# Cross-attention in f32 on one core: queries that lead by two steps, a sliced first block, residuals fetched three ahead and three score buffers in turn

## The chip, the cores and the metric

The kernel runs on one core of a Trainium2 chip. The metric is the device time of one execution in microseconds (us). Three runs of the kernel before are given, and one more execution was profiled.

## The reference

There are 2 sequences of 2048 tokens with 640 channels, and a context of 154 rows of 1024 channels for each. The context's first 77 rows are text and its last 77 rows an image prompt. Each kind has its own key and value weights. There are 20 heads of 32 channels. Every head takes two softmaxes over 77 keys each, one for either kind, and the two results are added. All of it is in f32.

```python
q = split(x @ Wq.T)
k, v       = split(text @ Wk.T),    split(text @ Wv.T)
k_ip, v_ip = split(ip @ Wk_ip.T),   split(ip @ Wv_ip.T)
out = attend(q, k, v) + attend(q, k_ip, v_ip)     # softmax(q k^T / sqrt(32)) v
return merge(out) @ Wo.T + bo + x
```

## The kernel before

Inputs come with the contracted dimension first (the launch code transposes them on the host), so tiles hold channels on the partitions. The 4096 tokens are four blocks `j` of 1024, and the 640 channels are five chunks `c` of 128, that is of four heads. A step `m` is one chunk of one block: `m = 5 j + c`, 20 steps in all, and a 21st that only finishes. The schedule is manual: each engine runs its instructions in the order in which the program text emits them, so what is written earlier is queued earlier.

A step makes scores for its 8 token tiles in three groups of 3, 3 and 2 tiles (`GROUPS`). For each group:

- `scores` (L202): TensorE (PE) multiplies queries by keys into four of the eight PSUM banks, `LOW` or `HIGH`. Groups 0 and 1 come at the start of the step, group 2 in its middle.
- `take` (L214): ScalarE (ACT) copies the banks to a buffer `pb` in SBUF. There is one buffer for each group, used again in each step.
- `maxima` (L221, L222): VectorE (DVE) takes the row maxima, GpSimd (POOL) subtracts them.
- `exponential` (L228) on ACT, `sums` (L235, L237) on DVE, `normalise` (L242) on POOL.
- `transpose` (L248) on DVE writes the probabilities, 32x32 blocks transposed, to `tT`.

In the next step `attend` (L260) multiplies values by `tT` into the `LOW` banks, and `take_attention` (L272) copies the result to `aT`. The output product is an object `Out` for each 128 channels by 512 tokens: `fetch` loads its residual from x (L290), `step` does one of its five matmuls (L295), `store` adds product, bias and residual on DVE (L306) and sends the sum out (L309). `fill(n)` does n such matmuls, and `flush` stores those that are complete. `fill` fetches a residual when its output is opened, and the next one with it.

PE's other work is placed into a step in two lists, so that PE has something to do while the softmax runs elsewhere: `after1` stands between the scores of groups 0, 1 and those of group 2, `after2` after `attend`. In block 0 these are the queries of step `m + 1` (`queries`, L177, in two halves `h` of 512 tokens), the values of this step and the keys of the next (`project_kv`, L135). From step 5 on they are query products and `fill(5)`. `turn_to` says which banks these products take in turn.

SP issues all DMAs in the order of the text. The head loads, slice by slice, the first chunk of `wq` and x's first half (L343, L344), then x's second half in one DMA (`load_x`, L164), the context into `wo_ct` (L348), the key and value weights into five slots (L126, `load_w`: each projection sends for the weights five further on) and the rest of `wq` (L355). `spread_v` (L157) copies the transposed values of a chunk to their places in 16 small DMAs; in steps 0 to 4 for sequence 0, in steps 6 to 10 for sequence 1, where they are issued after `take_attention`. x of the next block is loaded at `c == 2`.

Of the kernel before, what the change touches and what calls it, by code (L numbers as in the profile page):

```python
# [8 lines left out]
F32 = mybir.dt.float32  # L9
# [10 lines left out]
def kernel(  # L20
# [43 lines left out]
    OPEN = 4  # L64

    const = ctx.enter_context(tc.tile_pool(name="const", bufs=1))
    qpool = ctx.enter_context(tc.tile_pool(name="qpool", bufs=5))
    small = ctx.enter_context(tc.tile_pool(name="small", bufs=4))
    opool = ctx.enter_context(tc.tile_pool(name="opool", bufs=2))
    rpool = ctx.enter_context(tc.tile_pool(name="rpool", bufs=5))  # L70
    psum = ctx.enter_context(tc.tile_pool(name="psum", bufs=1, space=bass.MemoryType.PSUM))
# [5 lines left out]
    def turn_to(half, n=G):  # L77


        turn[:] = (half[: min(n, G) - 1] + half[-1:]) * 2  # L80

# [10 lines left out]

    pbs = [const.tile([P, n, G, LP], F32, name=f"pb_{t}") for t, n in GROUPS]
    for t in pbs:
        nc.gpsimd.memset(t[:, :, :, 2 * L :], 0.0)
# [92 lines left out]

    def keys_of(s):
        return pbs[s][:, :, :, : 2 * L]  # L190

    def rows_of(s):
        return keys_of(s).rearrange("p n g (t l) -> p (n g) t l", l=L)

# [14 lines left out]

    def take(s, ps):  # L210

        n = GROUPS[s][1]
        for g in range(G):
            nc.scalar.copy(  # L214
                keys_of(s)[:, :, g], ps[g][:, : n * 2 * L].rearrange("p (n l) -> p n l", n=n)
            )

    def maxima(m, s):
        n = GROUPS[s][1] * G
        mx = small.tile([P, n, 2], F32, tag=f"mx{n}", name=f"mx_{m}_{s}")  # L220
        nc.vector.tensor_reduce(mx, rows_of(s), AX.X, ALU.max)  # L221
        nc.gpsimd.tensor_tensor(  # L222
            rows_of(s), rows_of(s), mx.unsqueeze(3).to_broadcast([P, n, 2, L]), ALU.subtract
        )

    def exponential(m, s):
        e = keys_of(s).rearrange("p n g l -> p (n g) l")
        nc.scalar.activation(e, e, AF.Exp, scale=SCALE)  # L228
# [3 lines left out]
    def sums(m, s):  # L232
        n = GROUPS[s][1] * G
        den = small.tile([P, n, 2], F32, tag=f"den{n}", name=f"den_{m}_{s}")
        nc.vector.tensor_reduce(den, rows_of(s), AX.X, ALU.add)  # L235
        rden = small.tile([P, n, 2], F32, tag=f"rden{n}", name=f"rden_{m}_{s}")
        nc.vector.reciprocal(rden, den)  # L237
        rdens[s] = rden

    def normalise(m, s):  # L240
        n = GROUPS[s][1] * G
        nc.gpsimd.tensor_tensor(  # L242
            rows_of(s), rows_of(s), rdens[s].unsqueeze(3).to_broadcast([P, n, 2, L]), ALU.mult
        )

    def transpose(m, s):
        first, n = GROUPS[s]
        nc.vector.transpose(  # L248
            tT[:, first : first + n].rearrange("p n g k s -> p (n g k s)"),
            pbs[s].rearrange("p n g l -> p (n g l)"),  # L250
        )
# [63 lines left out]
    def fill(n, most=OPEN):  # L315


        while n > 0:
            o = next((o for o in opened if o.k < attended[o.j]), None)
            if o is None:  # L320
                v = len(finished) + len(opened)
                if v == NV or len(opened) == most or attended[outs[v].j] == 0:
                    return
                for o in outs[v : v + 2]:
                    o.fetch()
                opened.append(outs[v])
                continue
            o.step()
            n -= 1
            if o.k == NC:  # L330
                opened.remove(o)
                finished.append(o)
# [3 lines left out]
    def flush():  # L336
        for o in finished[len(stored) :]:
            o.store()
            stored.append(o)


    for k in range(NC):
        nc.sync.dma_start(out=wq[:, k, :P], in_=WqT[ts(k, P), :P])  # L343
        nc.sync.dma_start(out=xs[0][:, k, :TB], in_=xT[ts(k, P), :TB])  # L344
    load_x(0, 1)
    half = NCC // 2
    for k in (0, half):
# [4 lines left out]
        load_w()  # L352

    def load_wq(lo, hi):
        nc.sync.dma_start(  # L355
            out=wq[:, :, lo * P : hi * P],
            in_=WqT[:, lo * P : hi * P].rearrange("(k p) o -> p k o", p=P),
        )

    load_wq(1, 2)  # L360
    load_w()
    load_w()
    load_w()
    load_wq(2, NC)
    nc.sync.dma_start(out=bo_sb, in_=bo.rearrange("(c p) -> p c", p=P))
    turn_to(HIGH)
    for h in range(NH):
        queries(0, h)
    for t in range(2):
        project_k(0, t)  # L370

    for m in range(NM + 1):
        j, c, _ = block_of(m)
        new = m < NM
        old = m >= 1
        last = m == NM - 1

        if m < NC:
            after1 = [lambda: queries(m + 1, 0)]
            after1 += [lambda t=t: project_v(m, t) for t in range(2)]  # L380
            after2 = [lambda t=t: project_k(m + 1, t) for t in range(2) if m + 1 < NC]
            after2 += [lambda: queries(m + 1, 1)]
        elif c == 0 and new:
            after1 = [lambda h=h: queries(m + 1, h) for h in range(NH)]
            after2 = [lambda: fill(NC)] * 2
        elif last:
            after1 = [lambda: fill(NC)]
            after2 = [lambda: fill(NC)] + [lambda: fill(NC - 1)] * OPEN
        elif new:
            after1 = [lambda: fill(NC), lambda: queries(m + 1, 0)]  # L390
            after2 = [lambda: fill(NC), lambda: queries(m + 1, 1)]
        else:
            after1 = after2 = [lambda: None]
        flush()
        if new:
            for g, half in ((0, LOW), (1, HIGH)):
                scores(m, g, half)
            for g, half in ((0, LOW), (1, HIGH)):
                take(g, half)
        turn_to(LOW, len(after1))  # L400
        if old:
            transpose(m - 1, 2)
        if new:
            maxima(m, 0)
            maxima(m, 1)
        if c == 2 and j + 1 < NBLK:
            for h in range(NH):
                load_x(j + 1, h)

        ahead = len(after1) - (c > 0 or m == 0)  # L410
        for work in after1[:ahead]:
            work()
        flush()
        if new:
            exponential(m, 0)
            sums(m, 0)
            normalise(m, 0)
        for work in after1[ahead:]:
# [9 lines left out]
        if new:  # L428
            take(2, HIGH)
            maxima(m, 2)  # L430
            exponential(m, 1)
            sums(m, 1)
            normalise(m, 1)
        if old:
            take_attention(m - 1, LOW)
            attended[(m - 1) // NC] += 1
# [8 lines left out]
        if new:  # L445
            exponential(m, 2)
            sums(m, 2)
            normalise(m, 2)
        after2[-1]()
        if m >= NC and c == 0:  # L450
            flush()
        if new:
            transpose(m, 1)
# [38 lines left out]
```

## Time and profile before

| | us |
|---|---|
| three runs, median (lowest, highest) | 549.3 (548.97, 550.48) |
| the profiled execution's own time | 550.32 |
| its span, first to last instruction | 548.5 |
| PE busy | 524.3 (96% of the span) |
| DVE busy | 378.3 (69%) |
| POOL busy | 350.7 (64%) |
| ACT busy | 245.1 (45%) |
| idle time of PE that a profile row gives to a DMA of x | 6.3 |
| idle time of PE given to the output addition (L306), two waits | 9.1 |

The span leaves out what lies around the first and last instruction, which is 1.8 us here. In the profile PE stands for matmuls and PEld for weight loads, which overlap them. An f32 matmul leaves two records. L and a number is the line of the kernel, and SPq is the queue of DMA issues on SP. The granted clock (PEclk) is the share of full speed that TensorE was given.

### The profile page before, as it was taken

The page shows a single profiled execution, that of the slowest core. Times are in us where ns is not written, and L with a number is a line of the kernel's source. Part 1 is how long each engine was busy: PE and PEld are TensorE (multiplying, and loading weights), DVE is VectorE, ACT ScalarE, POOL GpSimd, SP SyncE. Part 2 cuts the span into 40 slices and gives each one's busy share as a digit, 9 for nine tenths or more (in the row PEclk, how much of TensorE's full clock was granted, in tenths as well). Part 3 has the DMA queues.
Part 4 walks back from the last instruction along what each step waited for, and adds up shares of the span by engine and source line. Part 5 has one row for each costly group of instructions (what it writes and reads, how often), then busy time and mean ns, then how long its engine had stood idle before and what let it go on. Part 6 is the DMA issues. An engine that isn't in the chain of part 4 may idle for free.

```text
span 548.5 us, 12745 instructions
## 1 busy us (share of the span) xinstructions
PE 524.3 (96%) x5600; PEld 285.9 (52%) x5600; DVE 378.3 (69%) x285; ACT 245.1 (45%) x441; POOL 350.7 (64%) x129
## 2 busy tenths in 40 slices
PE   5999999999999999999969999999999999969997
PEld 2676676866455445554535455554545544434442
DVE  0077778777798787878667887878588787864121
ACT  1254565546544446454435355464445645450000
POOL 0077967869678795786739595876779668691000
PEclk9999999999999999999979999999999999969999
DMA  7964384400420532121031621111032111121141
GB/s 267 305 185 104 87 271 106 126 17 20 166 78 29 176 127 84 45 65 57 16 106 40 232 70 47 41 39 39 2 98 58 40 39 41 38 99 38 59 165 66
DMA packets 49768, 50.60 MB, mean 92 GB/s; under 512 B 5168, under 2 KB 33712, under 8 KB 49712
## 3 DMA queue, kind: packets, MB, share of 16 engines
q1 hardware_dynamic: 49712, 49.78, 30.2%
q8 instruction: 44, 0.72, 0.6%
q14 instruction: 12, 0.10, 0.1%
HBM read 36.00 MB, written 10.49 MB: 85 GB/s over the span
## 4 chain that ended last, share of the span: by engine, by line
PE 86%; POOL 3%; SPq 3%; DMA 2%; DVE 2%; ACT 1%; issue 1%; ACTq 0%; DVEq 0%; POOLq 0%
PE bank L295 31%; PE bank L177 28%; PE bank L260 13%; PE bank L202 9%; PE bank L135 6%; DMA aT<-in_L_xattn_Wk_ip_dram 2%; POOL pb L242 2%; POOL pb L222 1%; SPq L348 1%; SPq L157 1%; DVE den L235 1%; DMA res<-in_x_dram 1%; DVE mx L221 1%; ACT pb L228 1%; DVE ot L306 0%
## 5 line engine op out<-in xcount | busy, mean ns | idle before, releaser
L222 POOL TENSOR_TENSOR pb<-pb,mx 128x1848 f32<-128x1848 f32 (+1 forms) x60 | 175.6, 2941 | 110.9 <-DVE mx L221 110.9
L242 POOL TENSOR_TENSOR pb<-pb,rden 128x1848 f32<-128x1848 f32 (+1 forms) x60 | 176.2, 2942 | 39.9 <-DVE rden L237 29.7
L177 PE MATMUL bank<-x,wq 128*128 128x512 f32 x400 | 181.9, 603 | 6.3 <-DMA x<-in_x_dram 6.3
L295 PE MATMUL bank<-aT,wo_ct 128*128 128x512 f32 x400 | 182.4, 608 | 2.1 <-ACT pb L214 1.2
L235 DVE TENSOR_REDUCE den<-pb 128x24 f32<-128x1848 f32 (+1 forms) x60 | 111.6, 1859 | 73.3 <-ACT pb L228 73.3
L228 ACT ACTIVATE pb<-pb 128x1848 f32<-128x1848 f32 (+1 forms) x60 | 95.2, 1587 | 97.7 <-POOL pb L222 97.6
L221 DVE TENSOR_REDUCE mx<-pb 128x24 f32<-128x1848 f32 (+1 forms) x60 | 109.2, 1848 | 37.2 <-ACT pb L214 35.9
L177 PEld LDWEIGHTS bank<-x,wq 128*128 128x128 f32 x400 | 75.8, 192 | 99.5 <-issue 94.7
L295 PEld LDWEIGHTS bank<-aT,wo_ct 128*128 128x128 f32 x400 | 75.0, 193 | 95.5 <-issue 85.0
L248 DVE STREAM_TRANSPOSE tT<-pb 128x1920 f32<-128x1920 f32 (+1 forms) x60 | 115.6, 1931 | 7.5 <-POOL pb L242 5.2
L214 ACT COPY pb<-bank 128x462 f32<-128x462 f32 (+1 forms) x240 | 101.5, 528 | 25.0 <-PE bank L202 15.8
L260 PE MATMUL bank<-tT,v 32*32 32x256 f32 x3200 | 71.8, 395 | 6.0 <-DVE ot L306 4.4
L185 ACT COPY qT<-bank 128x512 f32<-128x512 f32 x40 | 23.4, 585 | 95.5 <-PE bank L177 95.5
L202 PEld LDWEIGHTS bank<-kT,qT 32*128 32x128 f32 x1280 | 45.5, 186 | 32.4 <-issue 19.1
L306 DVE SCALAR_TENSOR_TENSOR ot<-bank,bo_sb,res 128x512 f32<-128x512 f32 x40 | 29.5, 739 | 47.1 <-PE bank L295 37.9
L202 PE MATMUL bank<-kT,qT 32*128 32x154 f32 x1280 | 55.4, 306 | 5.0 <-DVE ot L306 4.7
L260 PEld LDWEIGHTS bank<-tT,v 32*32 32x32 f32 x3200 | 46.8, 104 | 24.8 <-issue 6.6
L135 PEld LDWEIGHTS bank<-wo_ct,aT 128*128 128x128 f32 x320 | 43.1, 188 | 5.8 <-issue 3.4
L135 PE MATMUL bank<-wo_ct,aT 128*128 128x154 f32 x320 | 44.7, 295 | 1.0 <-ACT pb L214 0.5
L272 ACT COPY aT<-bank 128x256 f32<-128x256 f32 x80 | 24.3, 391 | 26.9 <-PE bank L260 26.9
L237 DVE RECIPROCAL rden<-den 128x24 f32<-128x24 f32 (+1 forms) x60 | 17.2, 286 | 2.1
L142 ACT COPY kT<-bank 128x154 f32<-128x154 f32 x10 | 2.9, 291 | 15.9 <-PE bank L135 15.9
(9 smaller groups left out, 7.3 us busy)
## 6 DMA issues: line engine op xcount, KB each, us to landing
res<-in_x_dram SPq DMA_DIRECT2D x40, 256.0 KB, 3.5
out_dram<-ot SPq DMA_DIRECT2D x40, 256.0 KB, 2.4
x<-in_x_dram SPq DMA_DIRECT2D x7, 1280.0 KB, 8.6
v<-vS SPq DMA_DIRECT2D x160, 20.0 KB, 1.8
aT<-in_L_xattn_Wk_dram SPq DMA_DIRECT2D x5, 512.0 KB, 6.8
aT<-in_L_xattn_Wk_ip_dram SPq DMA_DIRECT2D x5, 512.0 KB, 4.5
aT<-in_L_xattn_Wv_dram SPq DMA_DIRECT2D x5, 512.0 KB, 5.6
aT<-in_L_xattn_Wv_ip_dram SPq DMA_DIRECT2D x5, 512.0 KB, 4.2
```

Source lines behind the costliest of these rows:

```text
L135: nc.tensor.matmul(out, loaded[n][:, k, :], cT[:, k, :, t, :], start=(k == 0), stop=(k == NCC - 1))
L177: nc.tensor.matmul(pq, wq[:, k, ts(c, P)], xs[j % 2][:, k, ts(h, TB)], start=(k == 0), stop=(k == NC - 1),)
L202: nc.tensor.matmul(ps[g][:, ts(t, 2 * L)], qTs[(m, h)][g * D : (g + 1) * D, ts(st, P)], kT[g * D : (g + 1) * D, c, b].rearrange("p t l -> ...
L214: nc.scalar.copy(keys_of(s)[:, :, g], ps[g][:, : n * 2 * L].rearrange("p (n l) -> p n l", n=n))
L221: nc.vector.tensor_reduce(mx, rows_of(s), AX.X, ALU.max)
L222: nc.gpsimd.tensor_tensor(rows_of(s), rows_of(s), mx.unsqueeze(3).to_broadcast([P, n, 2, L]), ALU.subtract)
L228: nc.scalar.activation(e, e, AF.Exp, scale=SCALE)
L235: nc.vector.tensor_reduce(den, rows_of(s), AX.X, ALU.add)
L242: nc.gpsimd.tensor_tensor(rows_of(s), rows_of(s), rdens[s].unsqueeze(3).to_broadcast([P, n, 2, L]), ALU.mult)
L248: nc.vector.transpose(tT[:, first : first + n].rearrange("p n g k s -> p (n g k s)"), pbs[s].rearrange("p n g l -> p (n g l)"),)
L260: nc.tensor.matmul(pa[r][g * D : (g + 1) * D, : NT * D], v4[rows, c, g, k, :], tT[rows, :, g, k, :], start=(k == 0), stop=(k == NK - 1),)
L295: nc.tensor.matmul(self.po, wo[:, self.k, ts(self.o, P)], aTs[self.j % 2][:, self.k, ts(self.h, TB)], start=(self.k == 0), stop=(self.k == ...
```

## The change

It has four parts, and some reordering that goes with them.

1. Queries of a block's first half (`h = 0`) are made two steps ahead, those of the second half one step ahead as before (`LEAD`). The first products of the kernel become (0,0), (0,1) and (1,0).
2. In the head the five slices of `wq` are issued on ACT's queue, and SP issues both halves of x in five slices each. The second chunk of `wq` goes ahead of the context, and the third comes before the values' weights.
3. A residual is fetched at the store of the output three before it (`FETCH`); its pool has 4 buffers instead of 5.
4. The wide score buffers of groups 0 and 1 are three, taken in turn over the steps; group 2 keeps its own.

The reordering: x of the next block is loaded at `c == 1`. In steps 0, 18 and 19 (`short`) the second maxima come after the work of `after1` and the first two groups are exponentiated after the copies of group 2. In steps 5, 6, 11, 16 and 19 (`late`) the transposes of the step before come after the new maxima. In steps 1 and 2 all of `after1` is queued ahead of the first exponential. In step 18 the last output is stored at the step's end.

```diff
+    LEAD = (2, 1)
+    FETCH = 3
-    rpool = ctx.enter_context(tc.tile_pool(name="rpool", bufs=5))
+    rpool = ctx.enter_context(tc.tile_pool(name="rpool", bufs=4))
...
-        turn[:] = (half[: min(n, G) - 1] + half[-1:]) * 2
+        turn[:] = half[:1] if n == 1 else (half[: min(n, G) - 1] + half[-1:]) * 2
...
-    pbs = [const.tile([P, n, G, LP], F32, name=f"pb_{t}") for t, n in GROUPS]
+    wide = [const.tile([P, 3, G, LP], F32, name=f"pb3_{n}") for n in range(3)]
+    narrow = const.tile([P, 2, G, LP], F32, name="pb2")
...
+    def pb_of(m, s):
+        return narrow if s == 2 else wide[(2 * m + s) % 3]
...
+    def soften(m, s):
+        exponential(m, s)
+        sums(m, s)
+        normalise(m, s)
...
-                for o in outs[v : v + 2]:
-                    o.fetch()
+                outs[v].fetch()
...
         for o in finished[len(stored) :]:
             o.store()
             stored.append(o)
+            for o in outs[len(stored) : len(stored) + FETCH]:
+                o.fetch()
...
     for k in range(NC):
-        nc.sync.dma_start(out=wq[:, k, :P], in_=WqT[ts(k, P), :P])
-        nc.sync.dma_start(out=xs[0][:, k, :TB], in_=xT[ts(k, P), :TB])
-    load_x(0, 1)
+        nc.scalar.dma_start(out=wq[:, k, :P], in_=WqT[ts(k, P), :P])
+    for h in range(NH):
+        for k in range(NC):
+            nc.sync.dma_start(out=xs[0][:, k, ts(h, TB)], in_=xT[ts(k, P), ts(h, TB)])
+    load_wq(1, 2)
...
-    for h in range(NH):
-        queries(0, h)
+    for m, h in ((0, 0), (0, 1), (1, 0)):
+        queries(m, h)
+    turn_to(HIGH, NH)
...
+    def plan(m):
+        q = [lambda h=h: queries(m + LEAD[h], h) for h in range(NH)]
+        out = lambda: fill(NC)
+        if m < NC:
+            v = [lambda t=t: project_v(m, t) for t in range(2)]
+            k = [lambda t=t: project_k(m + 1, t) for t in range(2) if m + 1 < NC]
+            return q[:1] + v, k + q[1:]
+        if m == NM - 1:
+            return [out], [out] + [lambda: fill(NC - 1)] * OPEN
+        if m == NM - 2:
+            return [out], [out, q[1]]
+        if m % NC == 0:
+            return q, [out] * 2
+        return [out, q[0]], [out, q[1]]
+
+    def is_late(m):
+        return m in (NC, NM - 1) or (m > NC and m % NC == 1)
...
+        ahead = len(after1)
+        if ahead > 1 and 2 < m < NM - 2 and c > 0:
+            ahead -= 1
+        short = new and (len(after1) == 1 or m == 0)
+        late = is_late(m)
+        if old and not late:
             transpose(m - 1, 2)
         if new:
             maxima(m, 0)
+        if late:
+            transpose(m - 1, 1)
+        if new and not short:
             maxima(m, 1)
-        if c == 2 and j + 1 < NBLK:
+        if late:
+            transpose(m - 1, 2)
+        if c == 1 and j + 1 < NBLK:
             for h in range(NH):
                 load_x(j + 1, h)
...
         if new:
-            exponential(m, 0)
-            sums(m, 0)
-            normalise(m, 0)
+            if short:
+                maxima(m, 1)
+            else:
+                soften(m, 0)
...
             maxima(m, 2)
-            exponential(m, 1)
-            sums(m, 1)
-            normalise(m, 1)
+            if short:
+                soften(m, 0)
+                if old:
+                    take_attention(m - 1, LOW)
+            soften(m, 1)
...
-        after2[-1]()
-        if m >= NC and c == 0:
+        for work in after2[-1:]:
+            work()
+        if m >= NC and (c == 0 or m == NM - 2):
             flush()
-        if new:
+        if new and not is_late(m + 1):
             transpose(m, 1)
```

## The prediction

> **What bounds the kernel now.** I read the page first, then PE's own waits, then the timeline around each of those waits, then busy time and clock by stretches.
>
> From the page, the busy table and the rows of tenths:
>
> ```profile
> span 548.5 us, 12745 instructions
> PE 524.3 (96%) x5600; PEld 285.9 (52%) x5600; DVE 378.3 (69%) x285; ACT 245.1 (45%) x441; POOL 350.7 (64%) x129
> PE   5999999999999999999969999999999999969997
> PEclk9999999999999999999979999999999999969999
> ```
>
> PE (TensorE matmuls) is the bound; the others have a quarter or more of the span free. The dents are at the start, near slice 21 (274 to 288 us) and slice 36 (480 to 494 us), and the two later ones are dents of the granted clock too. So a gain can only come from these three places. PE's waits, longest first, say what ended them:
>
> ```profile
> PE bank L177 <- DMA x<-in_x_dram: 6.3, 2, 4.1
> PE bank L202 <- DVE ot L306: 4.7, 1, 4.7
> PE bank L260 <- DVE ot L306: 4.4, 1, 4.4
> PE bank L295 <- ACT pb L214: 1.2, 1, 1.2
> ```
>
> The timeline of the start (start, length, then what ran):
>
> ```profile
> 4.10 7.66 PE L177 MATMUL bank<-x,wq 128*128 128x512 f32 x10 [4.10 <-DMA x<-in_x_dram]
> 13.96 4.56 PE L177 MATMUL bank<-x,wq 128*128 128x512 f32 x10 [2.20 <-DMA x<-in_x_dram]
> 18.35 2.27 PE L135 MATMUL bank<-wo_ct,aT 128*128 128x154 f32 x16
> 21.03 2.37 PE L135 MATMUL bank<-wo_ct,aT 128*128 128x154 f32 x16 [0.40 <-DMA aT<-in_L_xattn_Wk_ip_dram]
> ```
>
> Ten records are one query product (five f32 matmuls, two records each). The first takes 7.66 us, later ones 4.5; then PE waits for x, then for key weights, and step 0 starts only at 23.78. Here PE follows the DMAs. The middle and the tail:
>
> ```profile
> 277.08 1.34 SPq L290 DMA_DIRECT2D res<-in_x_dram  x1
> 281.29 0.75 DVE L306 SCALAR_TENSOR_TENSOR ot<-bank,bo_sb,res 128x512 f32<-128x512 f32 x1 [4.56 <-DMA res<-in_x_dram]
> 282.09 1.90 PE L202 MATMUL bank<-kT,qT 32*128 32x154 f32 x18 [4.67 <-DVE ot L306]
> ...
> 482.64 2.08 DVE L235 TENSOR_REDUCE den<-pb 128x24 f32<-128x1848 f32 x1 [3.19 <-ACT pb L228]
> 484.97 0.65 DVE L306 SCALAR_TENSOR_TENSOR ot<-bank,bo_sb,res 128x512 f32<-128x512 f32 x1
> 485.68 5.17 PE L260 MATMUL bank<-tT,v 32*32 32x256 f32 x136 [4.36 <-DVE ot L306]
> ```
>
> In the middle (scores of step 11) a PSUM bank is not free because the output's last addition has no residual: its load stood on SP behind the 16 copies of v (L157, 266.8 to 277.0). In the tail (attention of step 18) the addition has its data but stands on DVE behind the sums of step 19, which wait for an exponential. Busy time and granted clock (the number before the DMA share) in stretches:
>
> ```profile
> 9.00:14.00 5.00, 2.80 (x6) 0.68 (x4) 0.00 (x0) 0.59 (x1) 0.00 (x0) 1.00 1.04 366
> 14.00:21.00 7.00, 6.63 (x26) 4.00 (x26) 0.00 (x0) 0.88 (x2) 0.00 (x0) 1.00 1.16 311
> 277.00:282.00 5.00, 0.43 (x14) 0.20 (x6) 0.71 (x2) 1.89 (x4) 2.15 (x1) 0.76 0.52 169
> 282.00:292.00 10.00, 9.91 (x34) 5.17 (x35) 8.21 (x6) 3.02 (x5) 4.45 (x2) 0.78 0.25 76
> 486.00:496.00 10.00, 10.00 (x144) 5.34 (x113) 5.43 (x4) 2.33 (x5) 7.94 (x3) 0.57 0.40 134
> ```
>
> After each long wait the clock is halved for a while: 10 x 0.22 = 2.2 us lost in the middle, 10 x 0.43 = 4.3 in the tail.
>
> **The change part by part.** *The head.* PE's work is the same in sum: the query product of step 1, first half, moves from inside step 0 to before the first key projections; each later step does the same product one step earlier, and step 18 has none. What counts is whether it fits where PE waits. Queries (0,0) start with x slice 0, whose issue is now SP's first (0.74 instead of 1.17): nearly as before, end 11.8 at the latest. SP's fourth x slice now waits until the first wq slice has landed [...]; that took 1.8 us from issue, so it goes out near 2.6, ahead of the 4.01 of before; behind it only x slices stand. Queries (0,1) need x's second half, landed at 13.9 in before; in slices all but the last matmul can be done by then: end 14.8. Queries (1,0) need 320 KB of wq now put ahead of the context: 0.33 MB at 311 GB/s is 1.1 us, so 15.1, and they run 4.4 us to 19.5. Keys: the first to 21.7, the second waits for its weights, which land 1.1 later than 21.03, so 22.1 to 24.5; the copy and 0.3 us more start step 0 at 24.8. That is 1.0 later than 23.78 with 4.5 us of work less outstanding: gain 3.5.
>
> [...] x's second half went as one 1280 KB DMA at up to 366 GB/s in that stretch, and is cut into five of 256 KB. [...] The trace has five x slices already, issued 0.95 apart, and the 16 engines are 0.8 to 1.0 busy from 3 us on with mixed slices at 275 GB/s (4 to 9 us): at that rate 1.31 MB costs 4.8 us instead of 3.6, so at most 1.2. I follow the row and take 0, since wq's narrow slices, not x's, are in that 275, and SP is spared five issues of 0.43.
>
> *Steps 0 to 2.* Value copies on ACT go before the exponential: 0.3 us of small PE waits (0.4 for vT) go. In step 0 the exponentials stand behind the third group's copies, so normalising starts 3.6 us later than now. By the durations (max 2.05, subtract 3.29, exponential 1.75, sum 2.08, multiply 3.29, transpose 2.12) step 0's last transpose ends 7.2 us into step 1, now 5.0; attention needs it at 11.4. Cost 0, cover 4 us; without it attention of steps 1 to 4 would wait.
>
> *Three wide buffers* free ACT's score copies from the previous transposes (1.6 and 0.6 us in steps 5 and 1): ACT is not on the path, 0. The moved transposes of steps 5, 6, 11, 16 end near 11 us into the step, the output addition after them 11.8 us, while attention asks at about 11.7: 0 to 0.3 each, taken as 0. Loads of the next x block go out one step earlier and still 46 us ahead of use; out stores behind them may be 7 us late, with 11 us between uses of an output buffer: 0.
>
> *The middle.* Each output now fetches the residual three further on, so both residuals of step 10 are issued in step 9, ahead of the 16 copies. The addition then runs when PE ends (about 277), and the scores' 4.7 us wait goes, and the 2.2 of clock: 6.9. Next late is that addition itself: 0 to 0.3.
>
> [...] Rows: 6.8 us at half clock after the middle's wait and 10.2 after the tail's (lost: 2.2 and 4.3 on work). [...]
>
> *The tail.* I walk DVE, POOL, ACT and PE from the start of step 18's scores (448.78, called 0) with the durations above. Step 18 has no query product for a first half; its output product is at 1.8 to 6.3, its addition now ahead of the second maxima (6.4 to 7.1), attention 7.1 to 10.5, output to 15.0, the last queries to 19.3. DVE is full here: transpose, then the second addition, ends 20.8, so the scores of step 19 wait 0.6. In step 19 both late transposes end at 28.2, the addition at 29.0, and attention, ready at 27.1, waits 1.9: a new wait, behind it the addition's followers on DVE (second maxima at 31.0). Attention ends 32.4, outputs (42 records) run to 50.5; the last transpose is done at 48.3, so the last attention starts at 50.5, with 2.2 us of cover. Now it starts at 510.93, i.e. 62.2 after. Less the 4.3 us of product moved to the head, the tail gains 62.2 - 4.3 - 50.5 = 7.4; I book 7.3. After it nothing changes (37.6 us to the end).
>
> Sum: 3.5 + 0.3 + 6.9 + 7.3 = 18.0. The profiled execution took 550.3 with a span of 548.5; its span would be 530.5 and its time 532.3. The runs' median is 549.3, 1.0 below that execution: 549.3 - 18.0 = 531.3.
>
> **The rivals.** *The head gives nothing.* If slices [...] hold x back, step 0 starts 4.5 us later and the moved product pays nothing: 534.8. For it: the engines are full, bytes decide. Against: PE idles there and needs only that the weights come by 22.
>
> *A new wait for a removed one, or the fetch does not do what it says.* If residuals still stood behind the v copies, the middle stays: 538.2. Against: the order of the new instructions puts both loads ahead. Nearer is the tail: 2.2 us of cover; a chain 4 us later makes the last attention wait 2 us, and if step 19's attention waits 4 instead of 1.9 the clock halves and 4 us go: about 537.
>
> *Slower: the softmax chain becomes the bound.* Place: steps 1 to 4. Step 0's late exponentials eat 2.2 of 6.4 us of cover; the chain recovers 1 us a step (22.3 against PE's 23.3). If the order costs over 4 us more than I walked, attention waits in each of these steps[...]. For it: DVE and POOL already trade off every step. Against: their rows give 22 us of chain.
>
> **How the numbers follow.** All stalls go as walked: 0.66, 531.3, own range 528 to 534. Head gives nothing: 0.13, 534.8. New wait or unchanged middle: 0.13, 537 to 538. Chain bound: 0.06, 555. Nothing gained: 0.02, near 549. The low end is the new tail waits not arising (2.5) and 1 us of the head: 527.5; the high end takes in the head and most of the new wait: 537.5. A difference under 0.3% (1.6 us) is about what a measurement of this kernel cannot tell from none: faster 0.92, same 0.02, slower 0.06.
>
> **What would show it.** Right: step 0's scores near 24.8 with three query products before them; no wait over 1 us at L202 near step 11 and PEclk 9 there; residual loads ahead of the v copies; a wait near 1.9 us at the attention of step 19, with the clock full; last attention to end 37 to 38 us. Wrong: scores of step 0 after 27; waits of PE for DVE's transposes in steps 1 to 4; a half clock anywhere after the first 12 us.

## The result: 541.7 us, and the profile after

| | before | after |
|---|---|---|
| runs, median (lowest, highest), us | 549.4 (548.97, 550.48) | 541.7 (540.79, 541.88) |
| profiled execution, us | 550.32 | 541.71 |
| its span, us | 548.5 | 539.9 |

The ratio is 0.985, with an interval of 0.984 to 0.987. The change gains 7.7 us of the 18.0 forecast, and 541.7 lies outside the range of 527.5 to 537.5. The last table of this section says where the 18.0 came and where not (bold).

The page of the changed kernel, busy table and rows of tenths:

```profile
PE 519.9 (96%) x5600; PEld 285.6 (53%) x5600; DVE 377.8 (70%) x285; ACT 245.3 (45%) x441; POOL 351.0 (65%) x130
PE   6999799999999999999999999999999999979997
PEclk9999999999999999999999999999999999999999
```

PE is still the bound. The dent in the middle is gone and that of the tail is smaller (7 instead of 6). There is a new one in the fifth slice (54 to 67 us), where before had 9. PE's waits, by what ended them (total us, times, longest):

```profile
PE bank L273 <- issue: 6.6, 4, 3.6
PE bank L181 <- DMA wq<-in_L_xattn_Wq_dram: 4.2, 1, 4.2
PE bank L273 <- DVE ot L319: 2.2, 1, 2.2
PE bank L210 <- DVE ot L319: 1.2, 1, 1.2
```

The scores of step 11, in before held up by 4.67 us and run at a granted clock of 0.50 (279.75 to 286.25 us), read in the timeline:

```profile
282.73 2.33 PE L210 MATMUL bank<-kT,qT 32*128 32x154 f32 x48
```

All 48 records run at once. The waits of 4.7 and 4.4 us for DVE have become 1.2 (in step 6) and 2.2 (in step 19). In their place stands a row of 6.6 us: PE idles *inside* the attention matmuls (L273, `attend`), and no engine, buffer or semaphore is named. In before it reads:

```profile
PE bank L260 <- issue: 1.2, 3, 0.5
```

Here is its largest case, in the timeline of step 1 (start, length, what ran):

```profile
48.36 2.33 SPq L168 DMA_DIRECT2D x<-in_x_dram  x2
56.70 3.33 PE L273 MATMUL bank<-tT,v 32*32 32x256 f32 x155
63.67 0.62 PE L273 MATMUL bank<-tT,v 32*32 32x256 f32 x5 [3.64 <-issue]
64.22 6.14 PE L139 MATMUL bank<-wo_ct,aT 128*128 128x154 f32 x32
```

155 of the 160 matmul records of one attention run, then PE stands still for 3.64 us, though the last five read no tile that the first 155 did not read. The next product takes 6.14 us instead of 4.38 (its length in the head). Busy time in stretches of the same place (PE, PEld, DVE, ACT, POOL; then granted clock, DMA share, GB/s), and last of before, whose step 1 starts 1.2 us earlier:

```profile
58.00:60.00 2.00, 2.00 (x102) 1.29 (x87) 0.00 (x0) 1.70 (x2) 2.00 (x2) 1.00 1.07 353
60.00:62.00 2.00, 0.03 (x2) 0.00 (x0) 1.92 (x1) 1.76 (x6) 1.52 (x1) 1.00 1.21 296
66.00:68.00 2.00, 2.00 (x9) 2.00 (x9) 1.97 (x3) 0.00 (x0) 2.00 (x1) 0.50 0.09 19
...
58.00:60.00 2.00, 2.00 (x81) 1.41 (x72) 1.97 (x4) 2.00 (x3) 1.01 (x1) 1.00 0.23 66
```

The DMA engines are full while PE has nothing (share 1.21 at 60 to 62 us, with 296 GB/s), and the clock is at 0.50 behind it. In before, where x of block 1 was loaded in step 2, the share was 0.81 at 56 to 58 us and then 0.23. My reading, which the experiments bear out, is that PE lacks its own program. The page has a row of instruction transfers:

```profile
q8 instruction: 44, 0.72, 0.6%
```

The row shows 44 transfers (0.72 MB: 16 KB each) and does not name the engine. If they bring PE's 11,200 records (matmuls and weight loads), each carries some 255: an estimate. An attention is 320 records in 3.38 us, so 255 of them last about 2.7 us. In the DMA trace PE goes on 2.35 to 2.6 us after such a load has begun, in each of the four gaps (begun at 458.45 and 481.35, on at 460.80 and 483.73, for the two of the tail). By these two times a load begun inside an attention comes just in time or just late: the gap is what is left of the 2.35 to 2.6 us when PE runs dry. In the tail the load begins 1.3 us before that; in step 1, with the DMA engines full (1.21), it is seen to begin at 61.1, a microsecond after it.

Counted from the trace in order of start, the gap of step 1 stands at PE's record 943 and those of steps 16, 18 and 19 at 9,099, 10,123 and 10,635. These last are 1,024 and 512 apart, multiples of 256, which bears out the 255: I take it that a border between two pieces comes about every 256 records. A steady step has 528, 16 more than two such pieces, so by this estimate the border creeps through the attention and gaps come in neighbouring steps. The tail:

```profile
456.49 3.25 PE L273 MATMUL bank<-tT,v 32*32 32x256 f32 x145
460.80 0.66 PE L273 MATMUL bank<-tT,v 32*32 32x256 f32 x15 [1.06 <-issue]
...
479.42 3.27 PE L273 MATMUL bank<-tT,v 32*32 32x256 f32 x147 [2.17 <-DVE ot L319]
483.73 0.66 PE L273 MATMUL bank<-tT,v 32*32 32x256 f32 x13 [1.04 <-issue]
```

The attentions of steps 18 and 19 each stop for a microsecond. The 2.17 is the new wait that the prediction walked to 1.9. The last attention starts at 502.54.

The account, from the starts of the scores of step 0, 2, 11, 18 and of the last attention in both timelines:

| stretch | before | after | gain | forecast |
|---|---|---|---|---|
| start to step 0 | 23.8 | 25.0 | -1.2 | -1.0 |
| step 0 to step 2 | 44.8 | 49.6 | **-4.8** | +0.3 |
| step 2 to step 11 | 207.5 | 208.2 | -0.7 | 0 |
| step 11 to step 18 | 172.6 | 166.6 | +6.0 | +6.9 |
| step 18 to last attention | 62.2 | 53.2 | **+9.0** | +11.8 |
| last attention to end | 37.6 | 37.4 | +0.2 | 0 |
| sum | | | 8.6 | 18.0 |

The forecast's 11.8 is its tail (7.3) and the product moved to the head (4.5). Half of the 9.4 that are missing lies in step 1, and some 30% in the tail.

### The profile page after: what moved, and what is told of

It reads as the page before. It is cut to its first block, busy times and chain, and to the rows that moved or that the text cites. A ratio compares the mean times of both kernels' runs of the same rounds, so it can differ in the third digit from the quotient of the medians.

```text
span 539.9 us, 12723 instructions
## 1 busy us (share of the span) xinstructions
PE 519.9 (96%) x5600; PEld 285.6 (53%) x5600; DVE 377.8 (70%) x285; ACT 245.3 (45%) x441; POOL 351.0 (65%) x130
## 4 chain that ended last, share of the span: by engine, by line
PE 90%; DVE 3%; issue 2%; ACT 2%; DMA 1%; POOL 1%; SPq 0%; ACTq 0%; DVEq 0%; POOLq 0%
PE bank L181 32%; PE bank L308 30%; PE bank L273 12%; PE bank L210 9%; PE bank L139 8%; DVE den L243 1%; DVE tT L261 1%; ACT pb L236 1%; DVE ot L319 1%; DMA wq<-in_L_xattn_Wq_dram 1%; POOL pb L250 1%; DMA res<-in_x_dram 1%; DVE mx L229 0%; POOL pb L230 0%; ACT pb L222 0%
## 5 line engine op out<-in xcount | busy, mean ns | idle before, releaser
L308 PE MATMUL bank<-aT,wo_ct 128*128 128x512 f32 x400 | 179.1, 599 | 0.9 <-ACT aT L285 0.9
L308 PEld LDWEIGHTS bank<-aT,wo_ct 128*128 128x128 f32 x400 | 73.7, 190 | 91.6 <-issue 83.8
L273 PE MATMUL bank<-tT,v 32*32 32x256 f32 x3200 | 70.7, 385 | 9.0 <-issue 6.6
L189 ACT COPY qT<-bank 128x512 f32<-128x512 f32 x40 | 23.4, 586 | 101.6 <-PE bank L181 101.6
L273 PEld LDWEIGHTS bank<-tT,v 32*32 32x32 f32 x3200 | 46.9, 103 | 27.3 <-issue 12.3
L210 PEld LDWEIGHTS bank<-kT,qT 32*128 32x128 f32 x1280 | 44.6, 184 | 29.2 <-issue 19.6
L139 PEld LDWEIGHTS bank<-wo_ct,aT 128*128 128x128 f32 x320 | 44.7, 194 | 4.8 <-issue 3.7
L139 PE MATMUL bank<-wo_ct,aT 128*128 128x154 f32 x320 | 45.9, 301 | 0.5 <-ACT pb L222 0.5
```

The source lines that it names most:

```text
L139: nc.tensor.matmul(out, loaded[n][:, k, :], cT[:, k, :, t, :], start=(k == 0), stop=(k == NCC - 1))
L210: nc.tensor.matmul(ps[g][:, ts(t, 2 * L)], qTs[(m, h)][g * D : (g + 1) * D, ts(st, P)], kT[g * D : (g + 1) * D, c, b].rearrange("p t l -> ...
L273: nc.tensor.matmul(pa[r][g * D : (g + 1) * D, : NT * D], v4[rows, c, g, k, :], tT[rows, :, g, k, :], start=(k == 0), stop=(k == NK - 1),)
L308: nc.tensor.matmul(self.po, wo[:, self.k, ts(self.o, P)], aTs[self.j % 2][:, self.k, ts(self.h, TB)], start=(self.k == 0), stop=(self.k == ...
```

## The experiments

All are the changed kernel with one edit, unless it is said otherwise. My theory: PE's instruction loads make the gaps, and x of block 1, moved one step ahead onto full DMA engines, makes the first one large. Rivals: the DMAs of x alone are the cause; the gap follows something in the attention's data; the softmax chain is late. Runs of before beside the experiments scattered from 545.1 to 553.4 us, where the first four lay between 549.0 and 550.5. One step of one kernel differs by up to 4 us between two profiles (step 6 below), so a part is read from its own step and not from the times.

**x of block 1 back in step 2.**

```diff
-        if c == 1 and j + 1 < NBLK:
+        if c == (2 if j == 0 else 1) and j + 1 < NBLK:
```

> The changed kernel, with x of block 1 loaded at step 2 as before instead of step 1 (later blocks keep step 1 of their block). Theory: PE's 3.64 us gap in the attention of step 1 is PE's own instruction load (the 16 KB transfer that the profile counts as queue q8) standing behind x's 2.6 MB and the weights on full DMA engines. Then the gap falls under 0.6 us, the clock is not halved after it, the scores of step 2 start 4 to 5 us earlier (near 70 instead of 74.7), and the time is 536.5 to 538 us. Rival 1, the gap stands at a place in the instruction stream and not at a load: it stays over 2 us and the time stays at 541.7. Rival 2, the gap moves to step 2 with the load: the same time, gap at the attention of step 2.

Measured: 539.2 us, ratio 0.980 (0.977 to 0.984); expected 536.5 to 538. This interval touches that of the change, so the step says more than the time. The timeline of step 1:

```profile
60.99 0.62 PE L273 MATMUL bank<-tT,v 32*32 32x256 f32 x5 [1.65 <-issue]
```

The gap falls from 3.64 to 1.65 us, after the same 155th record (under 0.6 was expected), and step 1 from 29.1 to 27.1. In six other profiles below, with x loaded in step 1 and the border at this place, it is 3.2 to 3.6, so the load of x makes 1.6 to 2.0 us of it. The rest stays, the half clock with it (0.50 in 64 to 66 us), so the moved load is not the whole cause.

**The same program shifted by 128 records.** 32 small matmuls in the head, whose result nothing reads:

```diff
+    for n in range(32):
+        nc.tensor.matmul(banks[0][:D, :D], wq[:D, 0, :D], xs[0][:D, 0, :D], start=True, stop=True)
```

> The changed kernel with 32 more matmuls of 32x32 by 32 in the head, after the three query products, into a bank that is free; their result is not used. They are 128 more matmul and weight-load records, half of what I take one instruction load to bring (11200 records over 44 loads is 255 each). Theory: the gaps of about 1 us inside the attention of steps 15 to 19 lie where the border of two loads falls early in an attention, which has 320 records in 3.3 us; a step has 528 records, that is 16 more than two loads, so the border drifts by 16 records a step. Half a load of shift then takes the gaps out of steps 16, 18 and 19 (3 to 4 us gained) and puts them some eight steps earlier, into steps 7 to 11 (3 to 4 us lost), with 1.5 to 3 us for the added matmuls: time 541.5 to 545 us. Rival, the gaps of steps 18 and 19 come from the order of ACT and DVE in those steps: they stay there at 1.0 us each, and none appear in steps 7 to 11: time 543 to 545 us.

Measured: 540.9 us, ratio 0.983 (0.979 to 0.988), a little under the 541.5 to 545 expected. The gaps went where the shift puts the borders. Step 1 has none, though x is still loaded there: it takes 23.7 us instead of 29.1. Steps 16, 18 and 19 have none. New ones stand in steps 2 (behind the attention), 8, 9 and 11, in which nothing else was altered; in step 11 the border meets the load of x for block 3. Timeline, step 11:

```profile
300.15 0.71 PE L273 MATMUL bank<-tT,v 32*32 32x256 f32 x28 [1.97 <-issue]
300.79 6.26 PE L308 MATMUL bank<-aT,wo_ct 128*128 128x512 f32 x10
```

A gap of 1.97 us is followed by a product of 6.26 us instead of 4.56. A cause in the data or in the chain would not move with matmuls that nobody reads: what counts is the place in PE's program. The time is no better than the change's, since the new gaps and a wait of 2.0 us with a half clock behind it in step 6 (27.6 us for the step) take back what the others give. The run also tries the tail without gaps: step 18's scores start at 452.13, so those of step 19 come 19.29 us later, and the last attention 50.1 (at 502.21). The prediction had 19.3 and 50.5.

**Attention cut in two.** In steps 6 to 9, 11 to 14 and 16 to 19 a product stands between its second and third chunk, so that fewer records come in a row.

```diff
+            attend(m - 1, LOW, range(2))
+            after2.pop(0)()
+            attend(m - 1, LOW, range(2, NK))
```

> The changed kernel with the attention of steps 6 to 9, 11 to 14 and 16 to 19 cut in two parts (key chunks 0 and 1, then 2 to 4), and the first output product of after2 between them. No work is added. Theory of the instruction load: no stretch of 320 records in 3.3 us is left in these steps, so the gaps of 0.9 us in step 16 and 1.1 and 1.0 in steps 18 and 19 go; the last attention starts 3 us earlier relative to step 16, time 538 to 539.5 us. Rival, the gaps come from the order of ACT and DVE or from a bank: they stay, since banks and orders are the same but for the copies of attention, which come 4 us later: time 541.5 to 543 us.

Measured: 545.4 us, ratio 0.993 (0.989 to 0.996), slower than the change itself: expected 538 to 539.5. The gaps of steps 16, 18 and 19 did go (those of the uncut steps 1 and 15 did not), but each cut has a price that I had not seen. One steady step of this kernel, and an uncut attention of the changed one:

```profile
224.59 1.90 PE L273 MATMUL bank<-tT,v 32*32 32x256 f32 x64
226.42 4.56 PE L308 MATMUL bank<-aT,wo_ct 128*128 128x512 f32 x10
230.91 2.13 PE L273 MATMUL bank<-tT,v 32*32 32x256 f32 x96
...
223.84 3.38 PE L273 MATMUL bank<-tT,v 32*32 32x256 f32 x160
```

1.90 + 2.13 is 0.65 more than 3.38, and the step takes 24.17 us instead of 23.40. Over 12 steps that is 8 to 9 us, more than the gaps cost.

**The first residuals early.** Step 5 is the cold start of "three ahead": its residual is issued at 162.7 and lands at 165.7, and step 6 waits 1.2 us.

```diff
+            for o in outs[:FETCH]:
+                o.fetch()
```

(at the end of step 4, ahead of the load of Wo)

> The changed kernel with the first three residuals fetched at the end of step 4, ahead of the load of Wo. Theory: at step 5 fetching three ahead has no start, since the second output's residual is issued only after the first output is stored; PE's wait of 1.2 us for the output addition at the scores of step 6 goes, and the time falls by 1.0 to 1.3 us to about 540.5. Rival, DVE would be late there anyway since the first addition stands behind the sums: PE still waits 0.5 to 1 us and the time falls by less than 0.5 us.

Measured: 542.6 us, ratio 0.986 (0.982 to 0.990), no gain. Timeline of step 5:

```profile
156.29 8.82 PE L308 MATMUL bank<-aT,wo_ct 128*128 128x512 f32 x20 [1.75 <-ACT aT L285]
```

Step 6 falls from 25.1 to 23.5 us, but step 5 rises from 23.9 to 25.7. Wo goes out later (at 146.7), lands at 156.15, and the first output product waits for it; the profile names ACT. The wait only moved.

**No lead.** Queries one step ahead again, only two products in the head.

```diff
-    LEAD = (2, 1)
+    LEAD = (1, 1)
...
-    for m, h in ((0, 0), (0, 1), (1, 0)):
+    for m, h in ((0, 0), (0, 1)):
...
-            return [out], [out, q[1]]
+            return [out, q[0]], [out, q[1]]
```

> The changed kernel without the lead: the first half's queries are one step ahead again, as the second half's; the head makes only the products (0,0) and (0,1), and step 18 has its product for step 19 again. Head loads, fetching and all orders stay as changed. The prediction's step: the product of 4.5 us fits where PE waits for weights, so here step 0 starts at the same 24.5 to 25 but every later step up to 18 comes 4 us later relative to the end of its own work; step 18, where DVE is full, takes it back by only 0.6 us or so: 545 to 546 us. The added 20 records earlier or later also move the border of the instruction loads, plus or minus 2 us. Rival: if PE has no idle time left in the head with slices, step 0 starts 4 us earlier here (near 20.7) and the time stays within 1 us of 541.7.

Measured: 541.7 us, ratio 0.985 (0.980 to 0.990), the same as the change; expected 545 to 546. In the head PE waits 3.27 us for key weights in place of the product, and step 0 starts at 24.35, only 0.6 earlier: the product did fill idle time. Step 18 takes 23.7 us, 4.4 more than the 19.3 of a step 18 without a gap. But PE's program is 20 records off in steps 1 to 18. The gap of step 18 is gone, which was worth 1.6 us (20.87 against 19.29), and in step 19 a half clock (0.50 in 482 to 485 us) behind the wait of 2.17 us stands in place of the gap. Step 1, first in this kernel, then in before:

```profile
62.76 6.73 PE L139 MATMUL bank<-wo_ct,aT 128*128 128x154 f32 x27 [2.07 <-issue]
...
59.54 4.85 PE L135 MATMUL bank<-wo_ct,aT 128*128 128x154 f32 x32
```

The gap of this kernel stands at the same record 943, but that is now in the product behind the attention, and step 1 takes 28.9 us. The load begins 15.3 us into the step. In before the border lies there too: the same record comes 0.3 us late (the product takes 4.85 us instead of 4.38), as PE reaches it only 2.4 us after the load has begun. In the kernel with x back in step 2 it lies in the attention and is reached 0.85 us after the beginning, though the load begins at the same place of the step (13.7 us in; in before 13.8). So it was the lead that carried the border into the attention.

The profiles differ by 1.8 us in favour of the lead and the medians by 0. One part can't be valued here by taking it out alone: the edit moves the borders too.

**The head's DMAs as before.** `wq` and x in turn on SP, x's second half in one DMA, the lead kept.

```diff
-        nc.scalar.dma_start(out=wq[:, k, :P], in_=WqT[ts(k, P), :P])
-    for h in range(NH):
-        for k in range(NC):
-            nc.sync.dma_start(out=xs[0][:, k, ts(h, TB)], in_=xT[ts(k, P), ts(h, TB)])
+        nc.sync.dma_start(out=wq[:, k, :P], in_=WqT[ts(k, P), :P])
+        nc.sync.dma_start(out=xs[0][:, k, :TB], in_=xT[ts(k, P), :TB])
+    load_x(0, 1)
```

> The changed kernel with the head's first loads as before: wq slices and x slices in turn on SP, x's second half in one DMA; the lead of the queries and the rest of the head stay. The prediction took the slices and ACT's queue to let queries (0,1) run from about 12 to 15. With the second half in one piece they start at 14.0 and end at 18.3, queries (1,0) at 22.6, and the two key projections at 27: step 0 starts near 27 instead of 25.0, and the time is 543.5 to 544.5 us. [...]

Measured: 545.8 us, ratio 0.995 (0.992 to 0.997). The head of this kernel, and after "..." that of the changed one:

```profile
27.00 1.85 PE L210 MATMUL bank<-kT,qT 32*128 32x154 f32 x48 [0.38 <-ACT kT L146]
...
4.21 16.19 PE L181 MATMUL bank<-x,wq 128*128 128x512 f32 x30 [4.21 <-DMA wq<-in_L_xattn_Wq_dram]
24.99 1.85 PE L210 MATMUL bank<-kT,qT 32*128 32x154 f32 x48 [0.38 <-ACT kT L146]
```

With x's second half in one DMA PE waits 1.89 us for it, and step 0 starts at 27.00, as expected, against 24.99 with slices, where thirty records run without a wait. The slices and ACT's queue for `wq`, which this run takes out together, are worth 2.0 us at least: in the other kernels with this head and the same products step 0 started between 24.1 and 25.0. The rest of the difference in time is in other places of the profile (step 1 took 30.1 us).

**Steps 18 and 19 in the old order.** Neither short nor late.

```diff
-        return m in (NC, NM - 1) or (m > NC and m % NC == 1)
+        return m == NC or (m > NC and m % NC == 1)
...
+        if m in (NM - 2, NM - 1):
+            ahead = 0
-        short = new and (len(after1) == 1 or m == 0)
+        short = new and m == 0
```

> The changed kernel with steps 18 and 19 in the order of before: output product after the exponentials and sums of group 0, transposes of step 18 not deferred, attention copies after the second group. Theory: the attention of step 19 waits again 4 to 5 us for the output addition behind the sums, and at half clock after it, so that 5 to 8 us come back and one slice near 480 us shows a granted clock under 0.8: 546.5 to 549.5 us. Rival, with three buffers and the lead the chain of steps 18 and 19 is early enough in either order: within 1.5 us of 541.7.

Measured: 552.0 us, ratio 1.007 (1.004 to 1.010), slower than before and worse than expected. PE's waits:

```profile
PE bank L273 <- DVE ot L319: 12.4, 2, 6.2
```

The output addition stands on DVE behind sums that wait for an exponential, as in before, but now in both steps. By the order of the text step 18 has one product less ahead of it; that this is why it no longer covers it was not tried by itself. The new order of the two steps is worth 10 us, and without it the change is a loss.

**The kernel before, with residuals three ahead only.**

```diff
-                for o in outs[v : v + 2]:
-                    o.fetch()
+                outs[v].fetch()
...
+            for o in outs[len(stored) : len(stored) + 3]:
+                o.fetch()
```

> The kernel before with one part of the change: residuals fetched three ahead at the stores (its pool stays at 5). The prediction's middle: PE's 4.7 us wait at the scores of step 11 and the half clock after it go, 6 to 7 us; step 5 loses about 1 us since its second residual now comes late. 543 to 544.5 us, ratio to before 0.989 to 0.991. Rival, the residual still stands behind the copies of v: no change. The order of PE's instructions is that of before, so the instruction loads stay where they were.

Measured: 543.8 us, ratio 0.990 (0.985 to 0.994), as expected. The scores of step 11 run without a wait, and the step takes 24.0 us instead of 30.7. This small part alone brings 5.6 us where the whole change brought 7.7 (6.2 and 8.1 against the runs of before taken beside it). It pays the cold start too (step 6: 25.5 instead of 23.9). Its tail is untouched, with the same wait of 4.36 us in step 19, and yet not as long. The output product behind that wait, in the timelines of before and of this kernel:

```profile
490.78 20.22 PE L295 MATMUL bank<-aT,wo_ct 128*128 128x512 f32 x42
...
484.89 18.29 PE L295 MATMUL bank<-aT,wo_ct 128*128 128x512 f32 x42
```

The clock record has 10.2 us at half clock in before and 6.8 here (mean clock of the span 0.984 and 0.992), and the stretch from step 18's scores to the last attention is 59.6 us instead of 62.2. So the same wait of 4.36 us cost two different amounts of clock.

**Two wide buffers.** `pb_of` returns `wide[s]`. In the late steps the transpose of the step before then reads the new step's scores, since their copies come first in the text; this part of the computation is changed.

> The changed kernel with two wide score buffers instead of three, one for each group as before. The prediction took the third buffer at zero. Against that: in steps 5, 6, 11, 16 and 19 the transpose of the old group 1 now stands behind the new maxima, so the copies of the new group 1 wait for it until 7 us into the step, second maxima and subtraction come 2 us later, and the attention of the next step, or the last one, may wait. Theory: within 1 us in the middle, 1 to 3 us lost in step 19: 542 to 545 us. If it is within 0.5 us of the changed kernel on this chip, the third buffer is worth nothing.

Measured: 542.5 us, ratio 0.987 (0.983 to 0.991). I had expected a wait that this order does not have, so the run says little of the third buffer's worth. By the text the third buffer is what lets the transposes be put off at all; elsewhere its lack costs one wait of 0.8 us (step 1).

**The changed kernel again**, with the last of these runs.

> The changed kernel itself once more, so that the others of this set can be set against it on the same chip: 0.985 of before, the gap of the attention of step 1 over 3 us and gaps near 1 us in steps 16, 18 and 19.

Measured: 541.9 us, ratio 0.985 (0.980 to 0.990). The gaps are in steps 1 (3.2 us), 15, 16 and 18. Step 6 waits 2.1 us, has 6.8 us of half clock behind it, and took 29.2 us here against 25.1, where a wait of 1.2 left the clock full.

**Mended together.** x of block 1 in step 2; first residuals early, but behind Wo; attention cut as above, but only in steps 1, 16, 18 and 19; step 1 in the order of step 0.

```diff
-        short = new and (len(after1) == 1 or m == 0)
+        short = new and (len(after1) == 1 or m <= 1)
...
-        if c == 1 and j + 1 < NBLK:
+        if c == (2 if j == 0 else 1) and j + 1 < NBLK:
...
+        split = m in (1, 16, 18, 19)
...
+            for o in outs[:FETCH]:
+                o.fetch()
```

> The changed kernel with three repairs: x of block 1 loaded at step 2 instead of 1; the first three residuals fetched right after the load of Wo; and only the attentions of steps 1, 16, 18 and 19 cut in two parts with the next product between them (a key projection in step 1, for which step 1 also gets the order of step 0). By the single runs: step 1 is back at 24.5 us (4.6 us gained), the scores of step 6 to 7 gain 1.2, and steps 16, 18 and 19 gain 1.6 each less 0.65 for each cut: 541.7 - 4.0 - 1.2 - 2.9, about 533.5 us (532 to 535.5). Rival, the gaps come back at other places in the stream since the border has moved with the order: 536 to 539 us.

Measured: 534.9 us, ratio 0.974 (0.971 to 0.978), as expected. Step 1 takes 23.7 us, step 6 23.8, and of the row of 6.6 us without a releaser 0.3 is left. New are a wait of 1.3 us for a copy of values in step 3 and one of 2.4 us for DVE at the scores of step 19.

**The same, with two waits taken out.** In the cut steps ACT copies the attention after the exponential, and in steps 3 and 4 the value copies come first.

```diff
-        if ahead > 1 and 2 < m < NM - 2 and c > 0:
+        if ahead > 1 and NC < m < NM - 2 and c > 0:
...
-                if old:
+                if old and not split:
...
-            if not short:
+            if split or not short:
```

> The version with the three repairs, with two faults of it mended: where an attention is cut, its copies on ACT come after the second group's exponential instead of before it (in steps 18 and 19 they held it up by 3.4 us, and PE waited 2.4 us at the scores of step 19), and in steps 3 and 4 both value copies are queued ahead of the first exponential (PE waited 1.3 us for one in step 3). Expected 2.5 to 4 us faster than that version: 531 to 532.5 us, ratio to before about 0.968. Rival, the chain of step 19 just ends later elsewhere: 533 to 535 us.

Measured: 535.7 us, ratio 0.974 (0.970 to 0.978), no better; expected 531 to 532.5. The wait of step 3 went, that of step 19 became one of 1.8 us at its attention, and PE came to step 5 1.6 us earlier. There it waits 2.31 us for a copy of queries (L189), which stands on ACT behind an exponential that itself waits 4.13 us for POOL. That exponential starts at 135.6 us, and at 135.1 in the kernel without these edits: there the softmax chain is the bound, and what PE gained ahead of it is lost.

## Why the prediction was wrong

- **The step that failed: "Loads of the next x block go out one step earlier and still 46 us ahead of use … 0", and in the head "PE's work is the same in sum".** "Steps 0 to 2" were booked at +0.3 and measured -4.8. I asked when the moved load's data are used and not what else needs the DMA engines while it runs: PE's own instructions. And I counted a product moved to the head as time only, not as 20 records of PE's program ahead of all that follows. The lead carried the border at record 943 from the product behind the attention into the attention of step 1; the load of x then made the instruction load begin after PE had run dry (a gap of 3.64 us, and of 1.65 with x in step 2). Each alone lengthens the step (24.3 us in before): the lead with x in step 2 to 27.1, x in step 1 without the lead to 28.9, both together to 29.1. About 1.7 us of each is the half clock behind the gap (with the lead, the product behind it takes 6.14 us instead of 4.38), or more (6.8 us of half clock without the lead), so the two do not add up. The shifted kernel, with both and the border elsewhere, takes 23.7. The page of before had the row of instruction loads, and its waits 1.2 us of PE idle with no releaser inside the attention; I read neither.
- **The tail, 7.3, was mis-sized; its mechanism holds.** The last attention came 53.2 us after step 18's scores instead of 50.5, by two more gaps of the same kind. With the borders elsewhere it came at 50.1. The new wait was forecast at 1.9 and is 2.17 (1.41 in the shifted kernel, with 0.49 ahead of the scores, forecast at 0.6). The order of the steps is needed, as the run with the old one shows.
- **The middle was right.** Forecast 6.9; the kernel with this part alone has 6.7 in that step. The changed kernel shows 6.0 up to step 18, since a gap of 0.9 us fell into step 16. I overlooked the cold start in step 5 (1.2 us, in one run 2.1 and 6.8 us of half clock behind it).
- **The head's number was right, in part by luck.** Step 0 at 24.99, forecast 24.8, with three products before it. But the walk let queries (0,1), a product of 4.4 us, end 3.0 us after (0,0): the three ended at 20.4 instead of 19.5. That the second keys' weights were there by then (landed at 20.55, forecast 22.1) made up for it. SP's fourth x slice went out at 4.18 and not near 2.6, since the first slice of `wq` took 3.4 us to land and not 1.8 (SP waited 2.1 us for that DMA); it cost nothing. Cutting x's second half into five slices of 256 KB was booked at 0 and cost nothing that shows: the head gained 3.3 us (4.5 of work for 1.2 later), and with x's second half in one DMA it was 2.0 worse. The ten slices of x landed 4.1 us after their issue (median), the one DMA of 1,280 KB in before 8.5 us after its own.
- **The clock.** For the middle the loss read from the rows of before (6.8 us at half clock, 2.2 of work) held: 6.7 us came back, where 4.7 + 2.2 = 6.9 was forecast. For the tail it did not: behind the same wait the kernel with the residuals alone has 6.8 us and not 10.2, and loses 2.4 us less, 1.9 instead of 4.3. After a gap of 1.97 us, in step 11 of the shifted kernel, 6.26 - 4.56 = 1.7 us were lost, at a clock of 0.77, 0.50 and 0.87 in the three stretches of 2 us from 300 on. The stretches at half clock were of 6.8 and 10.2 us in the trace of before and of 3.4 us in that of the changed kernel, beside one in its last half microsecond. The wait's length alone does not set how long: 3.4 us after 3.64 us in the changed kernel, 6.8 after 3.39 in the one with the head's old DMAs (mean clock 0.996 and 0.993). The runs do not show what does.
- **The rivals.** The head did give its gain, and the chain did not become the bound of steps 1 to 4 (the 555 for it was an estimate of mine). "A new wait for a removed one" was the nearest by its kind, but I looked for it among engines and buffers. Its price of about 6 us was too small. Of the signs of being wrong, "a half clock anywhere after the first 12 us" came, at 65 to 68 us.

What stays open: what sets the moment at which PE's next load begins (1.3 us before PE runs dry in the tail, 0.85 in step 1 without x of block 1; the DMA share is 0.52 to 0.71 there, so other transfers may be in its way, but I did not take them out); and what part of the third buffer's worth is its own.

## What to carry to other kernels

When a transfer is moved, ask not only when its data are needed but what else passes through the DMA engines at the new time, the engine's own instructions included; the sign here was PE idle with no releaser for 0.9 to 3.64 us inside a dense run of small matmuls. A small edit (128 records in the head, or 20 without the lead) moved the gaps in the program behind it, so differences of 1 to 5 us between versions need the account by steps before they are put down to the edit. And an order that served in before can cost once work beside it is moved away: with the old order of its last two steps the changed kernel is slower than before.

## What the runs showed of the hardware

- The page shows 44 instruction transfers of 16 KB beside 11,200 records of PE; 255 records for each is an estimate from these two. The gaps stand at the same records in kernels that differ around them (943 and 9,099 with the lead and without), and 128 records more in the head moved them to other steps. A load begun 2.35 us before PE went on was too late by 1.06 us, in matmuls that use up 255 records in about 2.7 us.
- With the DMA engines full (share 1.07 at 58 to 60 us and 1.21 at 60 to 62) the load began at 61.1, after PE had run dry at 60.03, and the gap was 3.64 us.
- Half clock followed gaps of 1.65, 1.97 and 3.64 us (0.50 in 64 to 66, in 302 to 304 and in 66 to 68 us) and not one of 1.06 (clock 1.00 in 461 to 467 us). Between them it was not settled: the same wait of 2.17 us in step 19 left the clock full in the changed kernel (1.00 in 477 to 491 us) and at half for 3.4 us in its second profile.
- An attention in 32x32 tiles that was cut in two by a full product took 1.90 + 2.13 us, 0.65 more than the 3.38 in one piece.
